# A four-layer graph network on one core: layer 0 issued as rounds in source order, with the later pairs' steps at fixed places

## The chip, the cores and the metric

The kernel runs on one core of a Trainium2 chip. The core has five engines that run their own lists of instructions and wait for one another through semaphores: TensorE (PE, with its weight loads listed as PEld), VectorE (DVE), ScalarE (ACT), GpSimd (POOL) and SyncE (SP), which here only issues DMA transfers. The metric is device time in microseconds; lower is better. The times of before are nine runs, 984.51 to 986.85 with a median of 985.57.

## What is computed

`x` is [32, 512, 128]: 32 graphs of 512 nodes with 128 features, all with the same 512x512 matrix `adj`. Four layers follow one another, each on a layer norm without parameters and a relu. Layer 0 is where the change lies; the others are named because their steps are laid out around it.

```python
def _layernorm(x, axis=-1, eps=1e-5): ...
# layer 0
h = max(_layernorm(x), 0)
A = softmax(where(adj > 0, e[0][cumsum(adj > 0) - 1], -9e15), axis=1)
x = x + (A * I) @ (h @ W[0]) + (A * (1 - I)) @ (h @ W[1]) + bias
# layer 1: Chebyshev hops with adj, twice
h = max(_layernorm(x), 0)
x = x + relu(stack([h, adj^T h, 2 adj^T(adj^T h) - h, ...]) @ Theta1 + bias)
# layer 2: messages with adj * adj, then two projections
# layer 3: attention, exp(8 tanh(s / 8)) * adj, normalised by rows
```

## The kernel before

**Pairs.** Two graphs make a pair, sixteen pairs in all, `q` = 0 to 15. A pair's `x` stays in SBUF (`xt[q]`) through all layers. Pairs 0 to 7 are loaded at the start, the others by `loads` while layer 0 runs.

**Layer 0 of a pair** has these steps.

- Statistics: four `bn_stats` on DVE (L198), the root on ACT (L212), a reciprocal (L214) and the shift `sh` (L215) on DVE. The `sh` operation reads two SBUF tiles of 128x8. Pairs 0 to 3 use four POOL operations instead, a power among them (L207 to L210).
- Normalising: eight ACT operations (L228) make `h`.
- Transposing: pairs 0 to 2 through TensorE and ACT (L252, L255); later pairs by two stream transposes on DVE (L262), four DMA writes to HBM (L266) and one DMA read back (L269), which gives `hT`.
- Projection: sixteen TensorE matmuls (L369) into two banks `p_g`, and two ACT copies (L401) that give `g` = h W[1].
- Right blocks: four POOL subtractions of 128x256 (L294 to L297), which give `rt_g`. The product A x g is done as seven block products in place of eight (a Strassen scheme), and these are the sums of blocks of its right side. The sums of its left side, `sums_att`, are made once, with two more matrices (`adj`, `cheb`) prepared the same way for layer 1 by `sum_steps` (L287).
- Products: `products` walks `ORDER`, seven block products of eight matmuls (L323) into three banks: a (first and fifth product), c (second, fourth, sixth), d (third, seventh). In between come diagonal matmuls with `hd` (L674), `hT` scaled by the diagonal of A on POOL (L650), and an eighth group into a bank of its own, e.
- Evictions on DVE: `u_l` three times from a, c, c and once more from d (L683, L686, L691, L692), then four into `x` (L696, L699, L702, L709). POOL adds each `u_l` to a quarter of `x` (L684, L687, L693), and the bias to the first quarter (L665). A product into a bank that is in use waits for the eviction ahead of it: the fourth product (c) for L686, the sixth (c) for L691.
- The statistics of the new `x`, for layer 1, by `ln_stats`.

**What sets the order.** Up to the first steps of layer 0 the kernel is inside `tc.manual_schedule(...)`: TensorE, DVE, ACT and POOL issue in the order of the source. Behind that, a scheduler in the compiler chooses the order by its own model of time, from generators that the last loop of the function steps in turn: each `yield` ends a step. `layer0(q)` is in list q of `waiting`; `first[q]`, which does statistics, normalising, transposing and projection of a later pair, is put into lists 0, 1 and q - 4; `loads` eight pairs ahead; the last rows of `cheb` (`pieces[3]`) into list 1; the sums of `adj` and `cheb` (`late_sums`) into list 3. SP's list is always the scheduler's.

Buffers that limit how far a pair can run ahead: `h` three, `hT` four, `hb` (the stream transposes' output) two, `rt` two, `hd` two, `u` two, and eight PSUM banks.

Of the kernel before, what the change touches and what calls it, by code (L numbers as in the profile page):

```python
# [9 lines left out]
F32 = mybir.dt.float32  # L10
# [10 lines left out]
EPS = 1e-5  # L21
EARLY = 3


@with_exitstack
def kernel(
# [147 lines left out]
    nc.scalar.activation(prep.tile([P, 1], F32, name="powers"), eps, AF.Exp)  # L174
    minus_half = prep.tile([P, NT, 2], F32, name="minus_half")
    nc.vector.memset(minus_half, -0.5)
# [10 lines left out]

    def ln_stats(q, hold=False):
        for _ in stats_steps(q, hold):
            pass  # L190

    def stats_steps(q, hold=False, powers=False):


        st = stats.tile([P, NT, 2, 3], F32, tag="bn", name=f"bn_{q}", bufs=4)
        for k in range(NT):
            b, t = divmod(2 * k, NT)
            ins = nc.vector.bn_stats(st[:, k].rearrange("p e s -> p (e s)"),  # L198
                                     xt[q][:, b, t : t + 2, :].rearrange("p t f -> p f t"))
            if hold:  # L200
                tc.keep_in_program_order(ins)
        yield
        sd = stats.tile([P, NT, 2], F32, tag="sd", name=f"sd_{q}", bufs=4)
        rs = stats.tile([P, NT, 2], F32, tag="rs", name=f"rs_{q}")
        sh = stats.tile([P, NT, 2], F32, tag="sh", name=f"sh_{q}")
        if powers:
            nc.gpsimd.tensor_scalar(sd, st[:, :, :, 2], 1.0 / D, EPS, OP.mult, OP.add)  # L207
            nc.gpsimd.tensor_tensor(rs, sd, minus_half, OP.pow)
            nc.gpsimd.tensor_mul(sh, st[:, :, :, 1], rs)
            nc.gpsimd.tensor_scalar(sh, sh, -1.0, None, OP.mult)  # L210
        else:
            nc.scalar.activation(sd, st[:, :, :, 2], AF.Sqrt, bias=eps, scale=1.0 / D)  # L212
            yield
            nc.vector.reciprocal(rs, sd)  # L214
            nc.vector.scalar_tensor_tensor(sh, st[:, :, :, 1], -1.0, rs, OP.mult, OP.mult)  # L215
        shift[q] = sh.rearrange("p k e -> p (k e)")
        scale[q] = rs.rearrange("p k e -> p (k e)")
        if powers:
            yield
# [21 lines left out]

    def transposed_by_pe(h, name):
        hT = feature_major(name)
        for _ in pe_steps(h, name, hT):
            pass
        return hT

    def pe_steps(h, name, hT):
# [7 lines left out]

    def transposed(h, name):


        hb = late.tile([P, NQR, 2, NT, QR], F32, tag="hb", name=f"hb_{name}", bufs=2)  # L260
        for b in range(2):
            nc.vector.transpose(hb[:, :, b].rearrange("p j t r -> p t j r"),  # L262
                                h[:, b].rearrange("p t (j c) -> p t j c", c=QR))
        d = bounce.tile([NQR, QR, NQR, 2 * P], F32, tag="d", name=f"d_{name}")
        for i in range(NQR):
# [3 lines left out]
        nc.sync.dma_start(hT.rearrange("p i b n -> p (i b n)"), d.rearrange("j c i e -> (j c) (i e)"))  # L269
        return hT  # L270

# [18 lines left out]
    def right_blocks(half, name, engs):  # L290

        t = work.tile([P, 4, 2, D], F32, tag="rt", name=f"rt_{name}", bufs=2)
        b11, b12, b21, b22 = half(0, 0), half(0, 1), half(1, 0), half(1, 1)
        engs[0].tensor_sub(t[:, 0], b12, b11)  # L294
        engs[1].tensor_sub(t[:, 1], b22, t[:, 0])
        engs[2].tensor_sub(t[:, 2], b22, b12)
        engs[3].tensor_sub(t[:, 3], b21, t[:, 1])  # L297
        return {1: b11, 2: b21, 3: b22, 4: t[:, 3], 5: t[:, 0], 6: t[:, 1], 7: t[:, 2]}

# [72 lines left out]

    def right_of(q):
        g = early[q][1]
        return right_blocks(lambda J, b: g[:, 2 * J : 2 * J + 2, b, :], f"g_{q}", [nc.gpsimd] * 4)

    def pair_tile(name):
        return work.tile([P, 2 * N + 2 * NT], F32, tag="pair", name=name, bufs=5)[:, : 2 * N]


    early = {}

    def layer0_first(q):
        if q >= 4:
            ln_stats(q)
            yield
        h = normed(q)
        yield
        hT = (transposed_by_pe if q < EARLY else transposed)(h, f"hT0_{q}")
        yield  # L390
        if q >= EARLY:
            yield
        for _ in project_steps(q, hT):
            pass

    def project_steps(q, hT):
        g = pair_tile(f"g_{q}").rearrange("p (t b f) -> p t b f", t=NT, b=2)
        pg = [projected(f"p_g_{q}_{b}", (at(hT, b), w0[:, 1, :])) for b in range(2)]
        yield
        for b in range(2):  # L400
            nc.scalar.copy(g[:, :, b, :], pg[b])  # L401
        early[q] = hT, g

# [9 lines left out]
    def cheb_rows(i):  # L413
# [7 lines left out]
        nc.gpsimd.tensor_sub(cheb[:, i, blk(i)], cheb[:, i, blk(i)], ident)  # L421

    first = {q: layer0_first(q) for q in range(2, NQ)}


# [79 lines left out]
    ln = [stats_steps(q, powers=True) for q in range(4)]  # L505
    next(ln[0])
    next(ln[0])
    bk = prep.tile([P, NK], F32, name="bk")
    nc.vector.tensor_copy(bk, pb[:, :NK])
    for kk in range(NK):  # L510
# [4 lines left out]
                                accum_out=col_of[:, kk : kk + 1])  # L515
        next(ln[0], None)
    h = {q: normed_tile(q) for q in range(2)}
    hT = {q: feature_major(f"hT0_{q}") for q in range(2)}
    normal = [normed_steps(q, h[q]) for q in range(2)]
    turned = [pe_steps(h[q], f"hT0_{q}", hT[q]) for q in range(2)]  # L520
    project = [project_steps(q, hT[q]) for q in range(2)]
    next(pieces[0], None)
    for _ in normal[0]:
        pass
    next(pieces[1])
    next(pieces[1])
# [12 lines left out]
    for kk in range(NK):  # L539
        for i in range(3):  # L540
            nc.vector.tensor_scalar(at_part[:, i, kk, :], cols, col_of[:, kk : kk + 1],
                                    parts[i][:, kk : kk + 1], OP.is_equal, OP.mult)
    next(ln[1])
    next(ln[1])

# [68 lines left out]
    for t in range(NT):  # L614
        nc.tensor.matmul(p[:, blk(t)], ones, diag[:, t, :], start=True, stop=True)
    for q in (2, 3):
        next(ln[q])
        next(ln[q])
        next(ln[q], None)
    rights = {0: right_of(0)}  # L620

    th12 = const.tile([P, 2, D], F32, name="th12")
    nc.gpsimd.tensor_add(th12, th[:, 1:3, :], th[:, 3:5, :])
    for j in range(NT):
# [3 lines left out]
    nc.scalar.copy(adiag, p)  # L628
    next(pieces[2], None)
    next(project[1], None)  # L630
    next(first[2])
    for _ in sum_steps(attT, "att", nc.vector):
        pass
    by_source.__exit__(None, None, None)

# [17 lines left out]
    def loads(q):  # L653
        if q == NQ - 2:
            both = last.tile([P, 2, 2, NT, D], F32, tag="x", name="x_last")
            xt.extend([both[:, 0], both[:, 1]])
        for b in (2 * q, 2 * q + 1):
            tc.keep_in_program_order(load_x(b))
        yield

    def layer0(q):
        hT = early[q][0]
        hd = [straight(hT, b, adiag, f"hd_{q}_{b}") for b in range(2)]
        x11 = xt[q][:, 0, 0:2, :]
        nc.gpsimd.tensor_add(x11, x11, spread(b0, 2))  # L665
        right = rights.pop(q, None) or right_of(q)
        yield

        def x_of(I, b):
            return xt[q][:, b, 2 * I : 2 * I + 2, :]  # L670

        def diagonal(p, I, b, first):
            for i in range(2):
                nc.tensor.matmul(p[:, i * D : (i + 1) * D], hd[b][:, blk(2 * I + i)], w0[:, 0, :],  # L674
                                 start=(first and i == 0), stop=True, skip_group_check=True)

        u = work.tile([P, 3, 2, D], F32, tag="u", name=f"u_l0_{q}", bufs=2)
        held = {}
# [24 lines left out]

        for i, _ in enumerate(products(f"l0_{q}", by_token, sums["att"], right, evict)):
            if q == 0 and i == 4:
                yield
        p = bank(f"p_l0_{q}_e")
        diagonal(p, 1, 1, True)
        nc.vector.tensor_add(x_of(1, 1), p[:, :H].rearrange("p (i f) -> p i f", i=2), x_of(1, 1))  # L709
        ln_stats(q)  # L710

# [115 lines left out]

    def late_sums():

        for name, mat in (("adj", adj_s), ("cheb", cheb)):  # L830
            yield from sum_steps(mat, name)

    waiting = [[layer0(q)] for q in range(NQ)]
    next(waiting[0][0])
    next(waiting[0][0])
    next(first[2])
    next(first[3])
    next(first[3])
    for q in range(NQ // 2, NQ):
        waiting[q - NQ // 2].append(loads(q))  # L840
    waiting[0].append(first[4])
    waiting[1] += [first[2], first[3], first[5]]
    for q in range(6, NQ):
        waiting[q - 4].append(first[q])
    waiting[1].append(pieces[3])
    waiting[3].append(late_sums())

    waiting[-1].insert(0, layer1(0))
    waiting += [[layer1(q)] for q in range(1, NQ)]
    waiting[NQ + 5].append(square())  # L850
    waiting[-1].insert(0, layer2(0))
# [41 lines left out]
```

## Time and profile before

| what | before |
|---|---|
| median of nine runs | 985.57 us |
| the profiled execution | 985.83 us |
| its span | 983.9 us |
| TensorE busy | 966.4 us, 98% |
| granted TensorE clock | 0.999 |
| layer 0's pairs, first product of pair 0 to the first of layer 1 | 39.05 to 205.93 us |
| DMA engines' mean busy share, from the queues | 30.7% |

The profile is one execution on the chip. In its timeline a row has the start, the length, the engine, the line, the operation, its output and inputs, the shape, a count, and in brackets how long the engine stood idle before it and who ended that. A window row has a stretch, its length, the busy time of PE, PEld, DVE, ACT and POOL in that stretch with counts, the granted clock, and the DMA's share and rate. A waits row has who waited for whom, the sum, how often, and the longest. TensorE's matmuls are pipelined, so that the next one can start before the one ahead has ended: of eight 128x128 matmuls that take 1.06 us the next group starts 0.89 us after their start.

### The profile page before, as it was taken

The page shows a single profiled execution, that of the slowest core. Times are in us where ns is not written, and L with a number is a line of the kernel's source. Part 1 is how long each engine was busy: PE and PEld are TensorE (multiplying, and loading weights), DVE is VectorE, ACT ScalarE, POOL GpSimd, SP SyncE. Part 2 cuts the span into 40 slices and gives each one's busy share as a digit, 9 for nine tenths or more (in the row PEclk, how much of TensorE's full clock was granted, in tenths as well). Part 3 has the DMA queues.
Part 4 walks back from the last instruction along what each step waited for, and adds up shares of the span by engine and source line. Part 5 has one row for each costly group of instructions (what it writes and reads, how often), then busy time and mean ns, then how long its engine had stood idle before and what let it go on. Part 6 is the DMA issues. An engine that isn't in the chain of part 4 may idle for free.

```text
span 983.9 us, 16147 instructions
## 1 busy us (share of the span) xinstructions
PE 966.4 (98%) x5926; PEld 802.0 (82%) x5926; DVE 588.5 (60%) x1386; ACT 467.0 (47%) x1057; POOL 412.2 (42%) x551
## 2 busy tenths in 40 slices
PE   8998999999999999999999999999999999999998
PEld 4788999999999999999977777777667776777776
DVE  8678787656565555656576666565654444444444
ACT  3853547122232322337767545455574555444553
POOL 4888897851225312211244333444133332233322
PEclk9999999999999999999999999999999999999999
DMA  9265645412122131234433333222222121121111
GB/s 259 90 171 141 181 104 146 117 43 81 49 65 65 44 86 44 65 86 130 107 102 104 105 120 107 85 69 83 57 84 76 43 76 54 55 76 43 54 33 43
DMA packets 83022, 87.17 MB, mean 89 GB/s; under 512 B 6784, under 2 KB 73088, under 8 KB 82944
## 3 DMA queue, kind: packets, MB, share of 16 engines
q1 hardware_dynamic: 82944, 86.14, 30.7%
q8 instruction: 47, 0.77, 0.3%
q14 instruction: 31, 0.25, 0.1%
HBM read 44.70 MB, written 41.42 MB: 88 GB/s over the span
## 4 chain that ended last, share of the span: by engine, by line
PE 89%; POOL 3%; DVE 2%; DMA 2%; ACT 2%; SPq 1%; issue 1%; DVEq 0%; ACTq 0%; POOLq 0%
PE p_av L801 12%; PE p_l L369 11%; PE p_score L788 11%; PE p_msgT_c L316 4%; PE p_x2T_c L316 4%; PE p_x1T_c L316 4%; PE p_l_c L323 3%; PE p_feat L369 3%; PE p_x1T_a L316 3%; PE p_hv L369 3%; PE p_x1T_d L316 3%; PE p_x2T_a L316 3%; PE p_x2T_d L316 3%; PE p_msgT_d L316 3%; PE p_qkh L775 3%; PE p_msgT_a L316 3%
## 5 line engine op out<-in xcount | busy, mean ns | idle before, releaser
L228 ACT ACTIVATE h<-x,sh,rs 128x128 f32<-128x128 f32 x448 | 182.5, 483 | 69.6 <-PE p_x2T_d L316 43.4
L793 POOL TENSOR_TENSOR ex<-ex,adjTx 128x512 f32<-128x512 f32 x64 | 83.4, 1305 | 197.0 <-issue 147.4
L789 ACT ACTIVATE ex<-p_score 128x512 f32<-128x512 f32 x128 | 71.6, 588 | 122.7 <-issue 112.9
L801 PEld LDWEIGHTS p_av<-qkh_hv,ex 128*128 128x128 f32 x1024 | 118.4, 191 | 9.6 <-issue 7.2
L801 PE MATMUL p_av<-qkh_hv,ex 128*128 128x129 f32 x1024 | 120.3, 275 | 0.9 <-POOL qkh_hv L782 0.6
L788 PE MATMUL p_score<-qkh_hv,hT 128*128 128x512 f32 x256 | 115.2, 593 | 0.0
L262 DVE STREAM_TRANSPOSE hb_hT<-h 128x512 f32<-128x512 f32 x122 | 84.6, 701 | 25.7 <-ACT h L228 25.2
L793 DVE TENSOR_TENSOR ex<-ex,adjTx 128x512 f32<-128x512 f32 x64 | 45.9, 718 | 76.2 <-ACT ex L791 76.2
L198 DVE BATCH_NORM_STATS2 bn<-x 128x6 f32<-128x256 f32 x224 | 83.3, 419 | 1.7
L788 PEld LDWEIGHTS p_score<-qkh_hv,hT 128*128 128x128 f32 x256 | 46.2, 190 | 46.5 <-issue 45.0
L791 ACT ACTIVATE ex<-ex 128x512 f32<-128x512 f32 x128 | 76.6, 631 | 1.9
L294 POOL TENSOR_TENSOR rt_h<-h 128x256 f32<-128x256 f32 x16 | 11.7, 730 | 133.9 <-PE p_x2T_c L316 133.0
L294 POOL TENSOR_TENSOR rt_feat<-feat,feat 128x256 f32<-128x256 f32 x16 | 11.7, 728 | 128.1 <-ACT feat L744 128.1
L369 PE MATMUL p_l<-th,x1T 128*128 128x128 f32 x256 | 49.5, 275 | 0.0
L369 PE MATMUL p_l<-th,x2T 128*128 128x128 f32 x256 | 49.5, 275 | 0.0
L369 PE MATMUL p_l<-th,hs 128*128 128x128 f32 x256 | 49.5, 275 | 0.0
L369 PEld LDWEIGHTS p_hv<-vw,hT 128*128 128x128 f32 x256 | 33.6, 192 | 15.3 <-issue 8.1
L401 ACT COPY g<-p_g 128x512 f32<-128x512 f32 x32 | 18.3, 578 | 57.7 <-PE p_g L369 57.6
L650 POOL TENSOR_TENSOR hd<-hT,adiag 128x512 f32<-128x512 f32 x32 | 40.6, 1279 | 5.4 <-PE p_l_e L674 3.8
L648 POOL COPY hs<-hT 128x512 f32<-128x512 f32 x32 | 19.6, 614 | 54.6 <-PE p_l L369 40.4
L342 ACT COPY x1T<-p_x1T_a 128x256 f32<-128x256 f32 x16 | 6.0, 373 | 74.8 <-PE p_x1T_a L316 74.8
L369 PEld LDWEIGHTS p_l<-th,hs 128*128 128x128 f32 x256 | 40.0, 192 | 0.8
(246 smaller groups left out, 2188.6 us busy)
## 6 DMA issues: line engine op xcount, KB each, us to landing
d_hT<-hb_hT SPq DMA_DIRECT2D x244, 128.0 KB
hT<-d_hT SPq DMA_DIRECT2D x61, 512.0 KB
x<-in_x_dram SPq DMA_DIRECT2D x28, 256.0 KB
out_dram<-x SPq DMA_DIRECT2D x28, 256.0 KB
adj_s<-in_adj_dram SPq DMA_DIRECT2D x4, 256.0 KB
adjT_d<-adjT SPq DMA_DIRECT2D x1, 1024.0 KB
sq<-in_adj_dram SPq DMA_DIRECT2D x4, 256.0 KB
x_last<-in_x_dram SPq DMA_DIRECT2D x4, 256.0 KB
```

The costliest lines, as they stand in the source:

```text
L198: ins = nc.vector.bn_stats(st[:, k].rearrange("p e s -> p (e s)"), xt[q][:, b, t : t + 2, :].rearrange("p t f -> p f t"))
L228: nc.scalar.activation(h[:, b, t, :], xt[q][:, b, t, :], AF.Relu, bias=shift[q][:, i : i + 1], scale=scale[q][:, i : i + 1])
L262: nc.vector.transpose(hb[:, :, b].rearrange("p j t r -> p t j r"), h[:, b].rearrange("p t (j c) -> p t j c", c=QR))
L316: nc.tensor.matmul(p[:, :H], b[:, k, :], a[:, k, :], start=(first and k == 0), stop=(k == 1), skip_group_check=True)
L323: nc.tensor.matmul(p[:, i * D : (i + 1) * D], a[:, k, blk(i)], b[:, k, :], start=(first and i == 0 and k == 0), stop=(k == 1), skip_group_ ...
L369: nc.tensor.matmul(p[:, blk(t)], hT(t), w, start=(i == 0), stop=(i == len(terms) - 1))
L650: nc.gpsimd.tensor_mul(split(s), src, split(scale))
L788: nc.tensor.matmul(ps, hT[:, t, b, :], qkh, start=True, stop=True)
L789: nc.scalar.activation(ex[:, t, :], ps, AF.Tanh, scale=1.0 / (8.0 * math.sqrt(D)))
L791: nc.scalar.activation(ex[:, t, :], ex[:, t, :], AF.Exp, scale=8.0)
L793: eng.tensor_mul(ex[:, t, :], ex[:, t, :], adjTx[0][:, t, :])
L801: nc.tensor.matmul(po[:, i, : D + 1], ex[:, t, blk(i0 + i)], hv[:, t, :], start=(t == 0), stop=(t == NT - 1))
```

## The change

Layer 0's sixteen pairs become rounds, `round0(r)`, and the rounds 0 to 14 stand inside the manual schedule too, so that TensorE, DVE, ACT and POOL issue them in source order; only the last pair, `layer0_last`, is left to the scheduler, with layer 1. The generators are split into finer steps: `stats_steps` yields after each `bn_stats`, `turn_steps` after each stream transpose, `right_steps` after each subtraction. `go(steps, n)` runs n steps of a generator. A round r in the middle places

- at its start, the normalising of pair r + 4, the root for the statistics of pair r - 1's new `x`, and two of the four right blocks of pair r + 1,
- between the seven products, the four `bn_stats` of pair r + 5, the other two right blocks of pair r + 1, the two stream transposes of pair r + 3 with their DMAs, and the reciprocal and `sh` of pair r - 1,
- behind the last eviction, the root, reciprocal and `sh` of pair r + 5, the four `bn_stats` of pair r's own new `x`, the projection of pair r + 2, the bias and `hd` of pair r + 1, one step of the sums of `adj` and `cheb` (r = 4 to 11), and the loads of pair r + 8.

Round 0 has places of its own: the POOL statistics of pair 3 now follow the right blocks and `hd` of pair 0, and the statistics of pairs 4 and 5 stand among pair 0's products. The last rows of `cheb` are issued in rounds 0, 1 and 2.

```diff
-    def stats_steps(q, hold=False, powers=False):
+    def stats_steps(q, powers=False):
...
+            yield
...
+    def turn_steps(h, name, done):
...
+    def right_steps(half, name, engs, right):
...
+    def go(steps, n=99):
+        for _ in range(n):
+            if next(steps, steps) is steps:
+                return
...
+    def round0(r):
...
+        stats5 = ahead.get(r + 5, iter(()))
+        nxt = right_of(r + 1) if r + 1 < NQ else iter(())
+        if r == 0:
+            diagonal_of(0)
+            go(ln[3])
+            go(pieces[2])
+            h[3] = normed_tile(3)
+            normal3 = normed_steps(3, h[3])
+            go(normal3, 4)
+            go(ahead[4], 2)
+        else:
+            if r + 4 < NQ:
+                normalise(r + 4)
+            go(own[r - 1], 1)
+            go(nxt, 2)
+        for i, _ in enumerate(products(f"l0_{r}", by_token, sums["att"], now, evict)):
+            if i == 0:
+                if r == 0:
+                    go(ahead[4], 2)
+                else:
+                    go(stats5, 1)
+            elif i == 1:
+                if r == 0:
+                    go(stats5, 2)
+                else:
+                    go(nxt)
+                    if r + 3 < NQ:
+                        turn(r + 3)
+            elif i == 2:
+                go(stats5, 1)
...
+            elif i == 4:
+                if r == 0:
+                    go(turned[2], 1)
+                    go(turned[2])
+                    go(normal3)
+                    go(ahead[4], 1)
+                    go(stats5, 1)
+                else:
+                    if r + 3 < NQ:
+                        go(turn(r + 3))
+                    go(own.pop(r - 1))
+            elif i == 5:
+                if r == 0:
+                    turn(3)
+                else:
+                    go(stats5, 2)
...
+        own[r] = stats_steps(r)
+        if r == 0:
+            go(turn(3))
+            go(nxt)
+            go(own[r], NT)
+            go(ahead[4])
+        go(stats5)
+        if r > 0:
+            go(own[r], NT)
+        if r + 2 < NQ:
+            go(projection(r + 2))
+        if r == 0:
+            normalise(4)
+        if r < 2:
+            go(pieces[3], 1)
+        elif r == 2:
+            go(pieces[3])
+        if r + 1 < NQ:
+            bias(r + 1)
+            if r >= 4:
+                go(sums_ahead, 1)
+            diagonal_of(r + 1)
+        if r == 3:
+            nc.gpsimd.tensor_add(th12, th[:, 1:3, :], th[:, 3:5, :])
+        if r + NQ // 2 < NQ:
+            loads(r + NQ // 2)
...
+    for r in range(NQ - 1):
+        round0(r)
+    by_source.__exit__(None, None, None)
+
+    next_layer = layer1(0)
+    next(next_layer)
+    waiting = [[next_layer, layer0_last(), layer1(1)]]
```

## The prediction

> **What bounds the kernel now.** First the busy times (part 1 of the page), then the chain that ended last (part 4), then who waited on TensorE.
>
> ```profile
> PE 966.4 (98%) x5926; PEld 802.0 (82%) x5926; DVE 588.5 (60%) x1386; ACT 467.0 (47%) x1057; POOL 412.2 (42%) x551
> ...
> PE 89%; POOL 3%; DVE 2%; DMA 2%; ACT 2%; SPq 1%; issue 1%; DVEq 0%; ACTq 0%; POOLq 0%
> ```
>
> ```profile
> PE p_l_c L323 <- DVE u_l L686: 4.8, 3, 2.2
> PE p_adjT L407 <- DMA adj_s<-in_adj_dram: 3.9, 2, 3.5
> PE p_l_c L323 <- DVE u_l L691: 1.5, 2, 1.2
> PE p_msgT_c L316 <- POOL rt_feat L295: 1.4, 1, 1.4
> PE p_l_c L323 <- POOL rt_g L295: 1.0, 1, 1.0
> ```
>
> The reader is to see: TensorE is the bound, and its waits are few. p_l_c is layer 0's third bank; its three rows (4.8 + 1.5 + 1.0 = 7.3 us) are what a reordering of layer 0 can win. The start (3.9) and layer 2 (1.4) are not touched. Next, layer 0 cut at the starts of p_l_a, the first product of a pair (window, length, then busy time by engine):
>
> ```profile
> 39.05:52.78 13.73, 12.69 (x102) 11.54 (x101) 7.04 (x18) 9.69 (x21) 13.57 (x19) 1.00 0.26 86
> 52.78:67.29 14.51, 12.08 (x94) 10.74 (x93) 12.52 (x37) 9.82 (x26) 11.66 (x15) 1.00 0.63 171
> ...
> 77.11:88.39 11.28, 10.10 (x91) 9.90 (x89) 8.08 (x23) 5.11 (x14) 8.84 (x11) 1.00 0.70 198
> 88.39:100.32 11.93, 10.09 (x90) 9.89 (x89) 10.24 (x22) 4.59 (x12) 10.94 (x13) 1.00 0.52 145
> ...
> 110.15:119.98 9.83, 9.83 (x91) 9.83 (x89) 7.84 (x22) 4.73 (x13) 9.67 (x12) 1.00 0.61 170
> 196.80:205.93 9.13, 8.31 (x74) 8.12 (x73) 6.25 (x15) 0.30 (x1) 7.35 (x10) 1.00 0.02 4
> ```
>
> An undisturbed pair takes 9.83 us with TensorE full, at full clock. POOL (fifth figure) is nearly full too: 9.67. That matters below.
>
> **What the change removes.** In the order in which the built programs' instructions stand, TensorE's list is the same but for one matmul in the last pair; only the lists of the other four change. So TensorE's work stays, and the gain is the excess of the pairs over their undisturbed length. Pair 0: 13.73 - (9.83 + 0.88 for pair 2's TensorE transposes, 45.27 to 46.15, + 1.72 for the cheb matmuls, 51.06 to 52.78) = 1.30. Pair 1: 14.51 - 11.55 = 2.96. Pair 3: 1.45. Pair 4: 2.10. Pair 15 has no projection (1.79, 108.36 to 110.15): 9.13 - 8.04 = 1.09. Sum 8.9 us.
>
> Each of these has a cause that the new order takes away. Pair 0 waits for rt_g, which stood behind pair 3's statistics on POOL (two powers of 1.67); these now follow rt_g and hd. Pairs 1 and 3 wait while DVE sits in a stream transpose whose h is not ready (80.76, idle 1.24 for h); the transposes now take an h that was normalised a round earlier. Pair 15's u_l stood behind a sh of 1.31; now sh follows it. Pair 4 is this:
>
> ```profile
> 88.89 3.27 DVE L215 SCALAR_TENSOR_TENSOR sh<-bn,rs 128x8 f32<-128x8 f32 x2
> 92.08 0.41 DVE L683 TENSOR_TENSOR u_l<-p_l_a,b 128x256 f32<-128x256 f32 x1
> 92.59 0.43 DVE L686 TENSOR_TENSOR u_l<-p_l_c,u_l 128x256 f32<-128x256 f32 x1
> ```
>
> ```profile
> 87.48 2.53 POOL L650 TENSOR_TENSOR hd<-hT,adiag 128x512 f32<-128x512 f32 x2
> 89.94 0.75 POOL L294 TENSOR_TENSOR rt_g<-g 128x256 f32<-128x256 f32 x1
> 90.63 0.75 POOL L296 TENSOR_TENSOR rt_g<-g 128x256 f32<-128x256 f32 x1
> 91.31 0.75 POOL L295 TENSOR_TENSOR rt_g<-g,rt_g 128x256 f32<-128x256 f32 x1
> 92.14 0.73 POOL L297 TENSOR_TENSOR rt_g<-g,rt_g 128x256 f32<-128x256 f32 x1
> ```
>
> A sh of eight columns, 0.11 us when alone, takes 3.2 us and ends as POOL stops for a moment at 92.06, before an operation that needs the one ahead of it. It reads two SBUF operands while POOL works without a gap. Most sh that begin under a POOL operation wait only for that one: 0.58 at 54.91, 1.31 at 198.77. Of some seventeen that meet back-to-back POOL work in this trace, one waited for several.
>
> The page "SBUF — State Buffer" of the Trainium skill (section "SBUF: two separate sides") has a rule for this: a DVE operation with two SBUF inputs and a GpSimd one lock the same port pair for a whole instruction, and the other fully blocks. The 0.58 agrees; that it also loses at the next boundaries, as in the 3.2, the rule leaves open.
>
> **What the new order keeps in place.** Offsets in us from p_l_a, an undisturbed round. TensorE: second product ends 1.95, the fourth starts 2.68 and needs the second eviction; last diagonal ends 8.2, projections 9.99. POOL's list: two rt, two x adds, two rt, an x add, the bias, in pairs 4 to 11 one 128x512 of the late sums, two hd. From start to start 128x256 is 0.69, 128x512 1.23: 8 x 0.69 + 2 x 1.23 = 8.0, with a sum 9.2, under 9.83. DVE: eight evictions at 0.34 and eight statistics at 0.35 make 5.5, two transposes 1.24, two reciprocals and sh some 0.8: 7.5, under 9.83. ACT is 4.7. So no engine becomes the bound by sum; what decides is order. After the last eviction (8.25 to 8.6) DVE has reciprocal and sh (8.95) and four statistics (10.3), and the next first product is ready at 10.9: 0.6 spare. One statistic then stands between first and second eviction: 11.25 to 11.6, needed from 11.9. Covered; without that spare each us is TensorE's.
>
> SP: the transposes still issue four writes and one read per pair. A pair's second transpose at 6.2 is followed in the trace by the read's issue 3.9 later (50.80 to 54.65, estimate); I take 4.5 more to land, an estimate from the next projection's never waiting. That is 14.6, needed at 9.83 + 8.04 = 17.9. Pair 3's first use is tighter: transposed about 50.8, landed 59.2, needed about 60.5. The x loads come after the read, three rounds early.
>
> **What it adds.** (a) Pair 0: the four sums of attT on DVE (0.69 each, two SBUF inputs) now meet rt_g and hd on POOL instead of the power. Each can wait for one POOL operation, three times up to 0.74 less what DVE had spare; four statistics of pair 4 now stand around the first eviction (1.4). No row shows this pairing; bounds 0 and 3 (all of rt and hd, 4 x 0.69 + 2 x 1.23 = 5.2, less the 2 spare). I take 0.8, nearest the single waits. (b) Pair 1: the sh of pairs 4 and 5 fall under the two hd (1.28 each), first eviction about 1 late, 0.4 on TensorE; bounds 0 and 2.3 (the old stall). (c) The last cheb subtraction on POOL stands, in source order, after pair 2's last x add and waits for ACT's copy, which stands behind pair 4's g copies. By the lengths above pair 3 starts at 39.05 + 12.44 + 0.8 + 11.55 + 0.4 + 9.83 = 74.1; the g copies end 0.9 behind that (140.45 against 139.63 in the trace: 0.8), the cheb copy 0.6 later, near 75.6. POOL, free near 70, sits until then, and pair 3's bias, hd, rt and x adds slide by up to 5. hd just holds (75.6 + 0.46 + 0.69 + 1.23 = 78.0; the diagonal takes it at 74.1 + 4.5 = 78.6); the last x eviction of pair 3 comes about 2 late and pair 4's second eviction 0.6. I take 0.7; bounds 0 and 2.1, pair 4's old stall. (d) In the rounds with a late sum, sh waits for one 1.28 operation twice: up to 0.15 a round; in all 0.3, bounds 0 and 1.2 (eight rounds). (e) sh losing several boundaries: some 28 sh in layer 0 times 1 in 17, at 1 us mean on TensorE net of the spare: 1.0, after bounds 0 and the rival below. Layers 1 to 3 keep their lists but for a few neighbours: 0, bounds -1 and +1.
>
> Sum: -8.9 + 0.8 + 0.4 + 0.7 + 0.3 + 1.0 = -5.7 us. The profiled execution took 985.83 (span 983.9 and 1.9 around it), 0.3 over the median 985.57; span after 978.2, median **979.9**.
>
> **The rivals.** *All removed, nothing new*: 985.57 - 8.9 = 976.7. For it: every sum is under 9.83, pairs 5 to 14 already run so. Against: (a) and (c) can be seen in the order.
>
> *POOL starves sh.* In pairs 4 to 11 POOL's list from the third x add to hd (5.0 to 10.1) has no operation that needs the one ahead. The sh of the pair before is due at 6.4. If it loses every boundary, as at 88.89, it ends at 10.1; then four x evictions and statistics, the second sh (gap at 11.4), four statistics, first eviction, a statistic, second eviction: ends 14.6 against 12.5. That is 2.0 a round, 16 in eight rounds: 978.9 (without e) + 16 = **995**, slower. It decides from the fourth such round on (3.3 x 2.0 = 6.7). For it: the 3.2 us, and that before, sh fell where POOL stops for g. Against: sixteen of seventeen got in at the first boundary.
>
> Under the skill's rule as written (who starts first holds for one instruction) this rival is out, and (e) is zero: the sum would be 978.9.
>
> *The waits only move*: (a), (b), (c) at upper bounds, 3 + 2.3 + 2.1, and pair 3's read a little late: the gain falls to 1 or less, 984.6 to 986. For it: rounds 0 to 3 have the narrowest margins. Against: three margins must go at once.
>
> That the change does nothing is excluded by the four engines' lists.
>
> **How the numbers follow.** Forecast 0.59 (own range 977.5 to 982.5), all removed 0.15, waits move 0.11, starvation 0.15. A measurement can tell 0.2%, 2.0 us: faster is below 983.6. Forecast and all removed are faster, with 0.02 of the moved waits: 0.76; starvation with a little of the moved waits slower: 0.16; same 0.08. The range reaches from all removed to light starvation (four rounds, 978.9 + 8 = 987): 976.5 to 987, with some 0.15 above and 0.04 below.
>
> **What would show it.** Right: p_l_c's waits fall from 7.3 to about 2 us; rounds 5 to 14 at 9.83; span near 978 with TensorE's busy time unchanged. Step by step: pair 0's second product starts right behind the first; no transpose waits for h; POOL idle some 4 us before its last cheb subtraction; sh in layer 0 mostly under 1.3 us. Wrong: rounds 4 to 11 near 11.8 with sh of 3 us or more (starvation), or a new releaser for p_l_c or p_g in pairs 0 to 4.

## The result and the profile after

The kernel after takes 981.11 us, median of 9 runs (980.42 to 982.34), beside 985.23 us for the kernel before in 29 runs (983.75 to 987.27): a ratio of 0.9959, 95% interval 0.9950 to 0.9967, or 4.1 us less. The profiled execution of after took 980.2 us with a span of 978.2, against 985.83 and 983.9 before.

First the page of after: busy times, and the chain that ended last.

```profile
PE 966.1 (99%) x5926; PEld 801.6 (82%) x5926; DVE 594.5 (61%) x1386; ACT 467.5 (48%) x1057; POOL 412.8 (42%) x551
...
PE 93%; POOL 2%; DVE 1%; ACT 1%; issue 1%; DMA 0%; SPq 0%; DVEq 0%; POOLq 0%; ACTq 0%
```

TensorE's work is the same (966.4 before); its share of the chain rose from 89% to 93%. What it waited for in the kernel after (us in total, times, longest):

```profile
PE p_adjT L405 <- DMA adj_s<-in_adj_dram: 3.8, 2, 3.6
PE p_msgT_c L319 <- POOL rt_feat L300: 1.4, 1, 1.4
PE p_l_c L326 <- DVE u_l L696: 1.3, 1, 1.3
PE p_av L886 <- POOL qkh_hv L867: 0.6, 1, 0.6
PE p_l_c L326 <- POOL hd L636: 0.5, 1, 0.5
```

The waits of p_l_c in layer 0 fell from 7.3 to 1.8 us; the others moved by 0.1 us or less. The 0.5 us put down to `hd` are pair 4's fourth product, which doesn't read `hd`: the second eviction, `u_l` at L696, ended at 87.21 and `hd` at 87.26, and the profile names the later one. The excess of pairs 0 and 4 below is 0.23 us more than the wait in them (pair 0: 1.48 and 1.25), since the product behind a wait doesn't overlap the one ahead of it. Layer 0 of after, cut at the starts of p_l_a as before (stretch, length, busy time of PE, PEld, DVE, ACT, POOL, then granted clock, DMA share and rate):

```profile
38.83:52.74 13.91, 12.65 (x102) 11.54 (x101) 11.15 (x26) 11.04 (x25) 13.50 (x18) 1.00 0.26 85
52.74:64.39 11.65, 11.65 (x93) 10.66 (x92) 10.01 (x25) 8.66 (x24) 10.36 (x14) 1.00 0.60 163
...
74.21:84.04 9.83, 9.83 (x90) 9.83 (x89) 6.24 (x17) 5.24 (x13) 8.38 (x11) 1.00 0.60 162
84.04:94.57 10.53, 10.06 (x90) 9.90 (x89) 9.27 (x25) 4.86 (x12) 10.45 (x14) 1.00 0.55 151
94.57:104.52 9.95, 9.95 (x90) 9.90 (x89) 8.90 (x25) 4.76 (x12) 9.87 (x13) 1.00 0.58 159
...
191.64:199.97 8.33, 8.28 (x75) 8.11 (x73) 6.31 (x17) 0.30 (x1) 7.76 (x10) 1.00 0.19 67
```

Taken as excess over each pair's undisturbed length, in us:

| pair | before | forecast for after | after |
|---|---|---|---|
| 0 | 1.30 | 0.8 (a) | 1.48 |
| 1 | 2.96 | 0.4 (b) | 0.10 |
| 3 | 1.45 | 0 | 0 |
| 4 | 2.10 | 0.7 (c) | 0.70 |
| 5 to 14 | 0 | 0.3 (d) and 1.0 (e) | 0.57, in pairs 5, 7, 9 |
| 15 | 1.09 | 0 | 0.29 |
| sum | 8.9 | 3.2 | 3.1 |

From the first p_l_a to the first product of layer 1 it is 166.88 us before and 161.14 after, 5.74 less. The stretch ahead is 0.23 shorter, layers 1 to 3 are 0.24 longer: 5.7 in the span.

Pair 0 gained nothing. In the timeline of after, DVE, then POOL, then TensorE:

```profile
37.41 1.10 DVE L285 TENSOR_TENSOR sums_att<-sums_att,attT 128x512 f32<-128x512 f32 x1
38.44 1.21 DVE L285 TENSOR_TENSOR attT<-attT 128x512 f32<-128x512 f32 x1
39.57 1.22 DVE L285 TENSOR_TENSOR sums_att<-attT,sums_att 128x512 f32<-128x512 f32 x1
...
37.93 1.17 POOL L300 TENSOR_TENSOR rt_g<-g 128x256 f32<-128x256 f32 x1
39.06 1.18 POOL L300 TENSOR_TENSOR rt_g<-g,rt_g 128x256 f32<-128x256 f32 x1
...
42.93 1.13 PE L326 MATMUL p_l_c<-rt_g,attT 128*128 128x128 f32 x8 [1.25 <-DVE u_l L696]
```

The wait for rt_g is gone, and a wait for DVE's second eviction stands two products later in its place: the sums of attT, 0.69 us alone, and rt_g, 0.73 alone, take turns and each is stretched to 1.1 or 1.2. Which operations meet matters: the power of 128x8 (1.67 us on POOL), beside which the sums stood in the kernel before, had left them at 0.69.

### The profile page after: what moved, and what is told of

Its sections match the earlier page's. It is cut to its first block, busy times and chain, and to the rows that moved or that the text cites. A ratio compares the mean times of both kernels' runs of the same rounds, so it can differ in the third digit from the quotient of the medians.

```text
span 978.2 us, 16184 instructions
## 1 busy us (share of the span) xinstructions
PE 966.1 (99%) x5926; PEld 801.6 (82%) x5926; DVE 594.5 (61%) x1386; ACT 467.5 (48%) x1057; POOL 412.8 (42%) x551
## 4 chain that ended last, share of the span: by engine, by line
PE 93%; POOL 2%; DVE 1%; ACT 1%; issue 1%; DMA 0%; SPq 0%; DVEq 0%; POOLq 0%; ACTq 0%
PE p_av L886 12%; PE p_l L372 12%; PE p_score L873 11%; PE p_msgT_c L319 4%; PE p_x2T_c L319 4%; PE p_x1T_c L319 4%; PE p_l_c L326 4%; PE p_feat L372 3%; PE p_x1T_a L319 3%; PE p_hv L372 3%; PE p_x1T_d L319 3%; PE p_x2T_d L319 3%; PE p_x2T_a L319 3%; PE p_msgT_d L319 3%; PE p_msgT_a L319 3%; PE p_qkh L860 3%
## 5 line engine op out<-in xcount | busy, mean ns | idle before, releaser
L300 POOL TENSOR_TENSOR rt_h<-h 128x256 f32<-128x256 f32 x32 | 22.6, 726 | 133.4 <-PE p_x2T_c L319 133.0
L300 POOL TENSOR_TENSOR rt_feat<-feat,feat 128x256 f32<-128x256 f32 x16 | 11.7, 729 | 128.3 <-ACT feat L829 128.3
L209 ACT ACTIVATE sd<-bn,eps 128x8 f32<-128x8 f32 x60 | 17.9, 300 | 56.1 <-DVE bn L197 55.0
```

## The experiments

Layer 0's length (161.14 us in after) and the lengths of single pairs are compared, since most questions are about less than 1 us. Each kernel is the kernel after with the edit shown.

**e1_cheb_early.** The last cheb subtraction (step c) ahead of the x adds of its round.

```diff
+                    if r == 2:
+                        go(pieces[3])
                     if r + 3 < NQ:
                         go(turn(r + 3))
...
-        elif r == 2:
-            go(pieces[3])
```

> One edit to the kernel after: in round 2 (which ends with pair 4's... start) the last cheb subtraction on POOL and its neighbours stand after product 4 of the pair and no longer behind the projection. Theory (step c of the prediction: POOL sat 5.73 us for ACT's cheb copy and everything of POOL behind it slid): that idle falls under 1 us, the wait of the x eviction at 84.15 (1.33 us on POOL's x) goes, the pair that is 10.53 us long now takes 9.83 to 9.95, and the span of the first sixteen pairs shrinks by 0.6 to 0.7 us. Rival (the 0.70 us come from DVE's own order, POOL's idle is only beside it): the idle goes and the pair still takes 10.4 to 10.6. In the whole time both lie within what one run can tell, so the pair's length decides.

In the kernel after the chain is this (POOL, then DVE):

```profile
75.58 0.46 POOL L419 TENSOR_TENSOR cheb<-cheb,ident 128x128 f32<-128x128 f32 x1 [5.73 <-ACT cheb L418]
...
84.15 0.42 DVE L764 TENSOR_TENSOR x<-p_l_e,x 128x256 f32<-128x256 f32 x1 [1.33 <-POOL x L703]
```

and in e1_cheb_early the same two operations are

```profile
70.22 0.46 POOL L419 TENSOR_TENSOR cheb<-cheb,ident 128x128 f32<-128x128 f32 x1
...
82.93 0.42 DVE L766 TENSOR_TENSOR x<-p_l_e,x 128x256 f32<-128x256 f32 x1
```

Both waits are gone and pair 4 takes 9.83. Step (c) holds, mechanism and size. Layer 0 takes 160.79, only 0.35 less: the excess of pairs 5 to 11 grew from 0.57 to 0.95. The whole is 980.27 us in its single run, which can't be told from the kernel after.

**e2_stats4_behind.** Pair 4's statistics out of pair 0's first evictions.

```diff
-            go(ahead[4], 2)
...
-                if r == 0:
-                    go(ahead[4], 2)
-                else:
+                if r > 0:
                     go(stats5, 1)
...
             elif i == 3 and r == 0:
+                go(ahead[4], 4)
                 go(stats5, 1)
```

> One edit to the kernel after: in round 0 pair 4's four statistics (0.35 us each alone) stand behind the second eviction and no longer two ahead of the first and two between first and second. Theory (step a: what holds pair 0's second p_l_c product for 1.25 us is DVE's list of lengthened attT sums plus these statistics): the 1.25 us wait on u_l falls to 0 to 0.3 us; pair 0 gets 0.85 to 1.2 us shorter (13.91 to about 12.9), a little of it may be given back to the second p_g, which waits for the hT copies. Rival (the port alone: the four sums, 0.7 to 1.2 us each, already make DVE late): the wait stays at 0.7 us or more and pair 0 at 13.4 or more.

Pair 0 takes 12.80, as the theory said; pair 1 takes 12.78 in place of 11.65. Together 25.58 against 25.56: nothing was won. What the expectation lacked is in DVE's timeline of e2_stats4_behind, and TensorE's wait at its end:

```profile
50.23 0.71 DVE L259 STREAM_TRANSPOSE hb_hT<-h 128x512 f32<-128x512 f32 x1 [1.15 <-ACT h L225]
50.87 1.38 DVE L197 BATCH_NORM_STATS2 bn<-x 128x6 f32<-128x256 f32 x4
...
52.39 0.92 DVE L212 SCALAR_TENSOR_TENSOR sh<-bn,rs 128x8 f32<-128x8 f32 x1
...
53.46 1.07 DVE L212 SCALAR_TENSOR_TENSOR sh<-bn,rs 128x8 f32<-128x8 f32 x1
...
55.67 1.13 PE L326 MATMUL p_l_c<-rt_g,attT 128*128 128x128 f32 x8 [1.00 <-DVE u_l L696]
```

DVE stands at a stream transpose until ACT has pair 3's h, and the statistics and the two sh of step (b) follow. This chain does not depend on pair 0's wait: the same transpose starts 11.2 us behind the first product of pair 0 in both kernels (50.23 here, 50.01 in the kernel after). There pair 0's wait only covers it. So pair 0's 1.25 us can't be won by itself. Pair 4 took 11.70 here (see e4_sums_later). Further on, pair 8 lost 1.99 to a sh of 3.63 us at 122.40.

**e3_power_first.** Pair 3's statistics back ahead of rt_g on POOL, as in the kernel before.

```diff
-    go(ln[3], NT)
+    go(ln[3])
     go(right_of(0))
```

> Undoes one part of the change: pair 3's statistics go as a whole, powers included, ahead of the four rt_g of pair 0, as in the kernel before. Theory (the wait has only changed hands): the attT sums on DVE fall back to about 0.7 us each (they now run beside the powers and no longer alternate with rt_g and hd), DVE's wait of 1.25 us falls under 0.4, a wait of p_l_c for rt_g of 0.8 to 1.2 us comes back, and pair 0 keeps its length within 0.3 us of 13.91. Rival (POOL's order is a gain, and the kernel after loses pair 0's time for another reason): both waits add up and pair 0 takes 14.8 to 15.3 us.

In e3_power_first, DVE and TensorE in pair 0:

```profile
37.56 0.69 DVE L285 TENSOR_TENSOR sums_att<-sums_att,attT 128x512 f32<-128x512 f32 x1
38.17 0.69 DVE L285 TENSOR_TENSOR attT<-attT 128x512 f32<-128x512 f32 x1
...
41.12 1.16 PE L326 MATMUL p_l_c<-rt_g,sums_att 128*128 128x128 f32 x8 [1.05 <-POOL rt_g L300]
```

The sums are back at 0.69, the wait for rt_g is back at 1.05, DVE's is gone, and pair 0 takes 13.73 against 13.91. The two orders cost the same; the theory holds. From the start of the first sum to the start of the operation behind the fourth it is 2.56 us here and 4.06 in the kernel after: the pairing costs DVE 1.5. The kernel's 985.35 us comes from elsewhere: pair 4 took 11.69, and pair 5 13.56 behind a sh of 3.18 us that lost three POOL operations in a row: TensorE waited 1.86 and then ran at half clock for a while (last section).

**e4_sums_later.** The late sums from round 7 on.

```diff
-            if r >= 4:
+            if r >= 7:
                 go(sums_ahead, 1)
```

> One edit to the kernel after: the late sums on POOL (one operation of 128x512 a round) begin with round 7 instead of round 4. Theory (step d: in rounds with a late sum POOL's list is 9.2 us of 9.83 and sh waits there for 1.28 us operations): the pairs that are 9.95, 10.01 and 10.10 us long (5, 7 and 9) change: 5 and 7 go to 9.83, and the excess of pairs 5 to 9, 0.57 us now, falls to 0.3 or less, unless it only moves to the rounds behind 9. Rival (that excess has another cause, the pair of cheb products' aftermath or the transposes): the excess stays at 0.5 to 0.6 with the same pairs.

Pair 7 fell to 9.83, but the excess moved: pairs 5, 8 and 10 have 0.14, 0.29 and 0.28, 0.71 in all against 0.57. Putting the sums off wins nothing. Nor does the excess follow the sums alone: pair 5 keeps its 0.14 with no late sum ahead of it. In each pair that pays, here and in the kernel after, the sh that starts 0.95 us ahead of the pair took 1.20 to 1.38 us under one operation of 1.28 us on POOL, a late sum once and `hd` else; in pairs 6 and 8 of the kernel after, which pay nothing, it took 0.56 and 0.59. Towards the end the last pair met a sh of 3.43 us, which cost 1.6. The run showed something else. In the kernel after, pair 4's sh got in just ahead of hd (84.72, 0.17 us). Here, DVE and POOL at the same place:

```profile
84.61 1.33 DVE L212 SCALAR_TENSOR_TENSOR sh<-bn,rs 128x8 f32<-128x8 f32 x1
...
84.65 2.49 POOL L636 TENSOR_TENSOR hd<-hT,adiag 128x512 f32<-128x512 f32 x2
```

It started 0.04 us ahead of hd (0.03 in the kernel after, hd at 84.75) and waited for the first of them all the same; pair 4 took 11.71 in place of 10.53.

**e5_stats_late.** The statistics of pairs 4 and 5 behind pair 0's last eviction, as before.

```diff
-            go(ahead[4], 2)
...
-                if r == 0:
-                    go(ahead[4], 2)
-                else:
+                if r > 0:
                     go(stats5, 1)
...
-                if r == 0:
-                    go(stats5, 2)
-                else:
+                if r > 0:
                     go(nxt)
...
-            elif i == 2:
-                go(stats5, 1)
-            elif i == 3 and r == 0:
+            elif i == 2 and r > 0:
                 go(stats5, 1)
...
-                    go(ahead[4], 1)
-                    go(stats5, 1)
```

> Undoes one part of the change: the statistics of pairs 4 and 5 (eight of 0.35 us) stand in round 0 behind the last eviction and pair 0's own statistics, as in the kernel before. Theory (what made the kernel before wait in pair 1 was that list on DVE ahead of pair 1's first eviction): pair 0 loses its 1.25 us wait and takes about 12.8 us, pair 1 takes 14.4 to 15.5 us with a wait of p_l_c for u_l of 2.5 to 3.5 us; pairs 0 and 1 together 27.2 to 28.3 us against 25.56 in the kernel after, the old stall of pair 1 back. Rival (the prediction's reason: pair 1 waited because stream transposes found their h not ready, and that is cured either way): pair 1 stays at 11.6 to 12.8 us and the two pairs at 24.5 to 25.6 us.

Pair 0 takes 13.07, pair 1 15.04, together 28.11; in the kernel before they were 28.24. In e5_stats_late, DVE and then TensorE:

```profile
51.77 2.71 DVE L197 BATCH_NORM_STATS2 bn<-x 128x6 f32<-128x256 f32 x8
...
58.66 1.13 PE L326 MATMUL p_l_c<-rt_g,attT 128*128 128x128 f32 x8 [3.10 <-DVE u_l L696]
```

In the kernel before, DVE's list ahead of pair 1's first eviction, and TensorE's wait, were

```profile
52.70 2.08 DVE L198 BATCH_NORM_STATS2 bn<-x 128x6 f32<-128x256 f32 x6
54.69 0.25 DVE L214 RECIPROCAL rs<-sd 128x8 f32<-128x8 f32 x2
54.91 1.26 DVE L215 SCALAR_TENSOR_TENSOR sh<-bn,rs 128x8 f32<-128x8 f32 x2
...
57.77 1.16 PE L323 MATMUL p_l_c<-rt_g,attT 128*128 128x128 f32 x8 [2.15 <-DVE u_l L686]
```

So the old stall of pair 1 is a list of statistics ahead of its first eviction: six and three sh that met POOL there, twelve and two short sh in e5_stats_late. No stream transpose stands in that list of the kernel before. The placing alone is worth 2.55 us in the kernel after, close to half of the gain.

**e6_h_same_round, e7_turns_together, e8_both.** The two halves of what the change does to the transposes, undone one by one and together.

```diff
-            if r + 4 < NQ:
-                normalise(r + 4)
+            if r + 3 < NQ:
+                normalise(r + 3)
...
-        if r == 0:
-            normalise(4)
```

```diff
                     if r + 3 < NQ:
-                        turn(r + 3)
+                        go(turn(r + 3))
...
-                    if r + 3 < NQ:
-                        go(turn(r + 3))
                     go(own.pop(r - 1))
```

> Undoes one part of the change: each h is normalised on ACT in the round in which it is transposed, no longer a round ahead; the two stream transposes stay apart (one behind the second eviction, one behind the fifth). Theory: ACT's eight activations take 3.2 us from the round's start and the transposes ask for the first half late enough; the rounds 1 to 12 lose 0 to 0.4 us each, 0 to 4 us in all, with the first transpose's idle for h up to 1.2 us. Rival (h a round ahead is what cured pairs 1 and 3): pairs 1 to 3 lose 1.2 us or more each and p_l_c's wait for u_l grows by 3 us or more in all.

> Undoes one part of the change: both stream transposes of a pair stand together behind the second eviction (2 x 0.70 us on DVE ahead of the third); h stays a round ahead. Theory: with h ready, the third eviction is due only 1.8 us behind the second, so 1.4 us fit: rounds stay at 9.83 to 10.1 us and the whole at the kernel after's time within 1 us. Rival (the split is what helps): 0.3 to 0.6 us more in each of rounds 1 to 12, 4 to 7 us in all.

> Both of the two edits before at once, which is nearest to the kernel before: both stream transposes behind the second eviction, on an h normalised in the same round. Theory (a transpose that finds its h not ready holds all of DVE behind it, and only that makes a stall): the second transpose waits for ACT's eighth activation, the third and fourth evictions come late, and every round from 1 to 12 takes 0.45 to 0.8 us more: 5 to 9 us in all, far above the sum of the two single edits. Rival (ACT is early enough even so): no more than the sum of the two single edits within 1 us.

Layer 0 takes 161.18 in e6_h_same_round (0.04 more), 164.11 in e7_turns_together (3.0 more) and 170.24 in e8_both (9.1 more). An h normalised in the round of its transposes costs nothing as long as these stand apart. In e8_both, DVE and TensorE in pair 3:

```profile
80.92 0.71 DVE L259 STREAM_TRANSPOSE hb_hT<-h 128x512 f32<-128x512 f32 x1 [0.83 <-ACT h L225]
...
82.32 1.16 PE L326 MATMUL p_l_c<-rt_g,attT 128*128 128x128 f32 x8 [0.72 <-DVE u_l L701]
```

The 0.83 us for h is the wait that the kernel before has at the same place (its second transpose in pair 3, at 82.30, also 0.83). So either half is a cure for it, and only both undone bring it back. The theory of e7_turns_together (within 1 us) missed: neither expectation foresaw its 1.8 us in pair 1, nor that in e8_both TensorE waits longer for the read of hT (4.2 us, five times) than for that eviction (2.4, eight times). SP's lists tell why; in the kernel after, the transfers of pair 3 are

```profile
50.78 1.78 SPq L264 DMA_DIRECT2D d_hT<-hb_hT  x4
54.67 0.34 SPq L267 DMA_DIRECT2D hT<-d_hT  x1
```

and in e7_turns_together, with TensorE's wait,

```profile
51.01 7.11 SPq L264 DMA_DIRECT2D d_hT<-hb_hT  x6
58.30 0.34 SPq L267 DMA_DIRECT2D hT<-d_hT  x1
...
62.85 2.02 PE L372 MATMUL p_g<-w,hT 128*128 128x128 f32 x16 [1.46 <-DMA hT<-d_hT]
```

With pair 4's second transpose 1.8 us earlier, two of its writes (they wait for the second transpose) stand ahead of pair 3's read on SP, and the read is issued 3.6 us later. In later rounds of both runs a pair's read stands behind the first write of the next pair.

**e9_sh_on_pool.** The product that makes sh, on POOL.

```diff
             nc.vector.reciprocal(rs, sd)
-            nc.vector.scalar_tensor_tensor(sh, st[:, :, :, 1], -1.0, rs, OP.mult, OP.mult)
+            if pool:
+                nc.vector.tensor_scalar(sd, rs, -1.0, None, OP.mult)
+                nc.gpsimd.tensor_mul(sh, st[:, :, :, 1], sd)
...
-    ahead = {q: stats_steps(q) for q in range(4, NQ)}
+    ahead = {q: stats_steps(q, pool=True) for q in range(4, NQ)}
...
-        own[r] = stats_steps(r)
+        own[r] = stats_steps(r, pool=True)
```

> One edit to the kernel after: in layer 0 the two-input product that makes sh (28 times, 128x8) is computed on POOL, in its place in the order, from a reciprocal that DVE negates (one more DVE operation with a single input, some 0.1 us); DVE has no sh left that could wait under a POOL operation. Theory (what is left above 9.83 in pairs 5 to 9, 0.57 us, and what makes executions differ by up to 2 us, is DVE's sh waiting at POOL's boundaries): pairs 5 to 14 all take 9.83 (8.04 the fifteenth), no pair behind the fifth takes over 10.0, the whole 0.5 to 2 us under the kernel after. Rival (POOL's list is nearly full, 9.2 of 9.83 us in a round with a late sum, and two more operations of 0.2 us that wait for DVE stop it): POOL comes late with its x adds and hd, p_l_c waits for POOL in the rounds with a late sum, 0.3 to 1.0 us each, and the whole is 1 to 5 us over the kernel after.

The median is 983.52 us (10 runs), a ratio of 0.9980 to before, interval 0.9971 to 0.9990: 2 to 3 us over the kernel after, as the rival said; but p_l_c waited for DVE's `u_l` (3.2 us, seven times) and not for POOL. Pairs 6 to 10 take 10.34 to 10.37. In one of them, POOL and DVE:

```profile
126.54 0.20 POOL L214 TENSOR_TENSOR sh<-bn,sd 128x8 f32<-128x8 f32 x1 [0.69 <-DVE sd L213]
...
125.72 0.42 DVE L768 TENSOR_TENSOR x<-p_l_e,x 128x256 f32<-128x256 f32 x1 [1.31 <-POOL x L707]
```

POOL waits for DVE's negated reciprocal and DVE for POOL's x add: two engines with full lists, coupled in a loop. Pair 4 still takes 10.52 with no sh left on DVE, so its 0.70 needs none.

**after_again and before_again.** Both kernels a second time, unchanged.

> The kernel after, unchanged, a second time. Theory (a sh that starts within 0.05 us of a POOL operation gets in or loses by chance, so executions of one program differ): the pairs 0 to 3 keep their lengths within 0.1 us, pair 4 takes either 10.5 (its sh gets in ahead of hd) or 11.7 us (it loses to it), and the profiled span is 978 to 981 us. Rival (the order in time is the same in each execution and the spread comes from elsewhere): all pairs keep their lengths within 0.1 us and the spans still differ by 1 us.

> The kernel before, unchanged, a second time. Theory (the 3.2 us sh in pair 4 was a chance, the stalls of pairs 0, 1 and 3 were order): pairs 0, 1 and 3 take 13.7, 14.5 and 11.3 us again within 0.1; pair 4 need not take 11.93 again, 9.9 to 12. Rival (its place in POOL's list decides): sh at the same place takes 3.2 us again and pair 4 11.9.

after_again: median 980.43 us of 4 runs, ratio 0.9949 (0.9934 to 0.9964). Pairs 1 to 10 have the same lengths within 0.04 and pair 4 10.52; pair 0 took 14.20 (0.29 more, outside the 0.1), the first product started 0.62 later, and the span is 0.85 longer. The rival's cause was partly right: some of the spread lies ahead of layer 0. before_again: pairs 0 and 3 as before; pair 4 took 10.48 in place of 11.93, its sh now 1.13 and 0.76. So the 3.2 us that the prediction read in the old profile is not there each time, and with it 1.45 of pair 4's 2.10 excess was a chance. Pair 1 took 15.60 in place of 14.51, which nobody expected (last section).

**best2.** e1_cheb_early and e2_stats4_behind together, and pair 0's own statistics put ahead of the transpose at which DVE stood idle:

```diff
         if r == 0:
+            go(own[r], NT)
             go(turn(3))
             go(nxt)
-            go(own[r], NT)
             go(ahead[4])
```

> Three edits to the kernel after together: the last cheb subtraction of POOL behind product 4 of round 2 (as in e1_cheb_early), pair 4's four statistics of round 0 behind the second eviction (as in e2_stats4_behind), and, new, pair 0's own four statistics ahead of pair 3's second stream transpose on DVE, which in e2_stats4_behind stood idle 1.15 us for its h while four statistics and two sh waited behind it ahead of pair 1's first eviction. Theory (pairs 0 and 1 hang on one chain on DVE, so that e2_stats4_behind alone only handed its 1.1 us from pair 0 to pair 1): pair 0 takes 12.8, pair 1 11.6 to 12.0, pair 4 9.83; 1.5 to 2 us under the kernel after, 976.3 to 977.5 in the span of an undisturbed execution and a median near 979. Rival (pair 1's list on DVE is as long as before whatever its order, or POOL's hd makes the sh lose as before): pairs 0 and 1 stay at 25.5 us together, and only the 0.7 us of pair 4 is won.

Median 984.04 us (11 runs), ratio 0.9983 to before (0.9974 to 0.9992): a miss. Pair 4 takes 9.83 and pair 0 13.05, but pair 1 16.04. In best2, SP and TensorE:

```profile
51.31 8.53 SPq L264 DMA_DIRECT2D d_hT<-hb_hT  x5
60.02 0.34 SPq L267 DMA_DIRECT2D hT<-d_hT  x1
...
64.50 2.02 PE L372 MATMUL p_g<-w,hT 128*128 128x128 f32 x16 [3.02 <-DMA hT<-d_hT]
```

One write of pair 4 now stands ahead of pair 3's read on SP, and the read goes out 5.3 us later than in the kernel after, though pair 3's transpose ended only 0.5 later. DVE did not win either: it stood 0.82 for ACT's root ahead of the reciprocal, sh took 1.21 under hd, and p_l_c still waited 1.0. Some of the median is the clock: seven of the eleven executions had a mean clock of 0.998 and took 984.5 us on average, the other four 983.0 (last section). A version that beats the kernel after was not found; e1_cheb_early, with one run, is the only candidate.

## Why the prediction was right, and where it was not

The time (979.9 forecast, 981.11 measured) and the span of the profiled execution (978.2 forecast and measured) came out close, but the exact span is luck: deviations cancelled, +0.7 in (a), +0.3 in pair 15, +0.3 in (d), -0.3 in (b), -1.0 in (e).

- **What the change removes.** Pairs 1, 3 and 4 lost their stalls as said. For pair 3 the cause named, a transpose whose h is not ready, is shown by e8_both. For pair 1 it was wrong: the wait of 2.15 for L686 was the list of statistics and sh (e5_stats_late), and only its second wait, 0.28 for L691, stood behind transposes. The stall was removed all the same, since the change also moves those statistics. "A round earlier" was not needed (e6_h_same_round). Of pair 4's 2.10, 1.45 was a chance of one execution (before_again). In pair 15 sh now follows the second eviction, as said, but four statistics stand ahead of the first (192.25 to 193.68), the likely reason for its 0.29.
- **(a), the sums of attT.** The mechanism was named, the size too small: taken at 0.8 by single waits, it is 1.48 of excess. The sums do not wait once; three of the four alternate with POOL operations. That pair 0's old wait would be a gain was the misjudged part: 1.30 went, 1.48 came (e3_power_first).
- **(b).** 0.10 in place of 0.4, because pair 0's wait covers it; uncovered it is 1.0 (e2_stats4_behind).
- **(c).** POOL sat from 69.9 to 75.6, where the prediction had it "free near 70" and the copy "near 75.6", and pair 4 paid 0.70. That was for a sh that got in; with the cheb subtraction where the change put it and sh on DVE, pair 4 took 10.3 to 10.7 in six profiles and 11.7 in three (e2, e3, e4). Both lie within the bounds, 0 and 2.1.
- **(d).** 0.57 for 0.3. The mechanism, a sh that waits for one POOL operation of 1.28 us, is in the traces, but `hd` does it as well as a late sum, and that the late sums cause it is not shown (e4_sums_later).
- **(e) and the starvation rival.** In the profile of after no sh lost more than one boundary (longest 1.37 us), so (e) was 0 there. Over the eleven profiles of the kernel after and its variants with sh on DVE, 199 sh in layer 0 took over 0.25 us, and five of them 2.2 to 3.6. They cost TensorE 2.0, 3.7 (with the half clock behind it), 0.4, 1.6 and 0.4 us, 0.7 per execution: the term's size is about right as a mean, but its working is not. 28 times 1 in 17 at 1 us is 1.6 and not 1.0, and in the trace of before only eleven of layer 0's 27 sh, and not seventeen, start while POOL works. One reading is off too: the sh of 1.31 at 198.77 began 0.06 us ahead of the end of one POOL operation and waited for the whole of the next. That a sh loses every boundary in each round did not happen.
- **SP.** The estimate of 4.5 us from the read's issue to use holds: 58.30 to 62.85 in e7_turns_together, 60.02 to 64.50 in best2. The list itself was taken as fixed by its source place, which the runs refute: two moves changed it, that of e7_turns_together (which e8_both shares) and that of best2. In the other variants its order in layer 0 is that of the kernel after.
- **From span to median.** The median missed by 1.2 us, probably for the other side of the same chances. The profiled execution of after is the quickest of its ten (spans 978.2 to 980.2), with pair 4's sh let in, no long sh and an early start; that of before held a long sh, which its second profile does not. Which of these each unprofiled execution had is open.

## What to carry to other kernels

When one engine is full and three others pass work around, a stall that is removed uncovers the next chain with nearly the same end: before a wait is priced, take away its cover on paper and see who is late then. One profile is one throw where two engines meet within some 0.05 us at a shared resource: a stall that such a meeting made is neither certain to be there nor certain to be gone. Moving a step by a microsecond can reorder a queue that a scheduler fills, so compare the lists of all queues, the DMA queue first.

## What the runs showed of the hardware that was not expected

**Half clock behind a wait, by chance.** In before_again, TensorE's wait of 2.17 us in pair 1 was followed by this (windows, the clock is the third figure from the end):

```profile
58.60:60.20 1.60, 1.60 (x8) 1.60 (x9) 0.71 (x1) 1.60 (x6) 1.60 (x3) 0.56 1.06 313
60.20:61.90 1.70, 1.70 (x10) 1.70 (x9) 1.44 (x3) 1.70 (x6) 1.09 (x3) 0.50 0.89 237
...
62.50:64.00 1.50, 1.50 (x16) 1.50 (x15) 1.29 (x4) 0.80 (x3) 0.04 (x1) 1.00 1.02 264
```

The first profile of before has the same wait, 2.15, and a clock of 1.00 behind it. Pair 1's 1.09 extra is this; in e3_power_first a wait of 1.86 was followed by 3.6 us at half clock too (3.4 in before_again), but the 3.10 of e5_stats_late and the 3.02 of best2's profile were not. Of 30 executions of the kernel before beside the experiments, 15 had a mean clock of 0.998 and took 985.95 us on average, the others 984.69; of 14 of the kernel after, all had 1.000. By these averages about 0.6 us of the measured 4.1 (half of 1.26) is the clock, a gain that the prediction did not have; that each of the fifteen met its half clock behind pair 1's wait is not shown. The page "TensorE: Matmul & The Clock Gate" of the Trainium skill (section "Part 1: The HAM clock gate (the "warmup" mystery)") has the clock at half after an idle window of about 3.4 us that runs freely, so that it falls differently in each run. Half clock for about 3.5 us, and by chance, agrees; that a wait of 1.9 us is enough is less than a whole idle window.

**A lock that is lost at a hair.** In nine profiles (after, after_again, e2 to e8) pair 4's sh started 0.03 to 0.05 us ahead of hd. In six it took 0.17 us, in three (e2, e3, e4) 1.33. The lead does not tell which: it was 0.03 in after and in e2_stats4_behind. Operations that read one SBUF tile into statistics, or transpose one, were not stretched beside POOL: bn_stats stayed at 0.35 each under hd. But e9_sh_on_pool's negated reciprocal, a tensor_scalar with one input, also took up to 0.69 us where it needs 0.13 alone. The page "SBUF — State Buffer" of the Trainium skill (section "SBUF: two separate sides") counts DVE operations in a two-port mode among those that take the shared ports, which agrees if this is one. Its rule that whoever starts first holds them for that whole instruction fits the turns in pair 0 only in part: one operation of each passed in 1.13 us, where their start-to-start times alone, 0.60 and 0.69, sum to 1.29. The five sh of 2.2 to 3.6 us, which lost three POOL operations or more in a row, it does not give.
